# Graph attention on one core: the last two batches of a scatter, summed chunk by chunk or two chunks in turn on column groups of the PE

## The chip, the cores and the metric

The kernel runs on one core of a Trainium2 chip. The metric is the device time of one launch in microseconds (us). Engines are named as in the profile: PE multiplies matrices (PEld is its weight load), DVE and ACT work on vectors, POOL issues the gathers, SP issues other transfers. PE writes only to PSUM, DVE and ACT read it. The PE's clock is throttled, and the profile lists the share of it that was granted.

## The reference

One layer of graph attention on 12500 nodes and 412500 edges, sorted by their target node `dst`, self loops included. With H = 4 heads of 32 values:

```
h   = relu(layernorm(x)) @ W_node.T            per node, 4 x 32
e   = edge_attr @ W_edge.T                     per edge, 4 x 32
att = leaky(sum(concat(h[src], h[dst], e) * a))
m   = max(segment_max(att, dst), 0)
ex  = exp(att - m[dst])
den = segment_sum(ex, dst) + (E - degree) * exp(-m)
out = x + segment_sum(ex / den[dst] * h[src], dst)
```

All is float32. The change concerns the last sum, of weighted rows `ex * h[src]` into the rows of their targets.

## The kernel before

**Chunks and batches.** The sorted edges are cut in 461 chunks of 896 edges (7 tiles of 128; the last chunk has 3 tiles). Eight chunks make a batch; there are 58 batches (`NBT`), numbered 0 to 57, and the last one has 5 chunks. A table in memory holds for each node its projected row, 140 values (4 heads x 35) and 4 more. `gather` (L495) fetches the rows of a batch's source nodes with one indirect transfer per tile into `hs`, from POOL, a batch ahead of the arithmetic.

**What is done with a batch.** `begin` (L509) makes the scores `z` on PE (L518, L521) and the matrices `hot` on DVE (L533): for each tile, 128 edges x 32, a one where an edge's target is the row of that number in the chunk's window of 32 nodes. `weigh` (L537) makes the exponentials `ex_ps` on DVE and ACT (L549 to L564), with a running maximum. `scatter` (L567) multiplies the gathered rows by them on DVE (L578, one instruction of 128x924 values per chunk) and sums them on PE (L586): `hot` of a tile is the stationary operand, the weighted rows are the moving one, and the tiles of a chunk accumulate in PSUM. In batches 0 to 55 three chunks share a matmul (96 x 420), of which only the diagonal blocks are used. In the last two batches, 56 and 57 (`step` 1), each chunk has its own matmuls, 32 x 140, 7 of them, in a PSUM tile `pa` of its own. The name `pa` has two buffers, which are taken in turn; a third tile has to wait until the first was read. A float32 matmul stands in the trace as two records, with two weight loads.

**Collecting and merging.** `collect` (L592) copies each chunk's 32 x 140 block as four blocks of 32 x 35, a head each, from PSUM into `r`: on ACT (L609), and for the last chunk of the last batch on DVE and ACT in turn (L607, L609). `merge` (L611) then scales and scans the chunks of one batch (of two batches, further ahead) on DVE and ACT and adds the result to `acc`. Where nodes are complete, `finish` (L696) divides, brings the four heads together with 16 small matmuls (L721) and stores rows. Those matmuls go to four column groups in turn: each has `tile_position=(0, s * W)`, and writes the PSUM rows `s * W` to `s * W + 31` for s = 0 to 3.

**What sets the order.** The order of instructions on each engine is that of the program (`manual_schedule`). In the main loop, round b issues `load` and `gather` of batch b + 1, `weigh` and `scatter` of b, `begin` of b + 1, `merge`, and `finish` of the nodes that are done. Waits between engines are placed by the framework from the tiles that the instructions read and write. At the end stand `scatter` of 56, `begin` of 57, `merge` and `finish`, then `weigh`, `scatter`, `merge` and `finish` of 57. Constants: `W` = 32 rows a window, `H` = 4, `AW` = 35, `HB` = 33, `G` = 3, `T` = 7.

Of the kernel before, what the change touches and what calls it, by code (L numbers as in the profile page):

```python
# [9 lines left out]
F32 = mybir.dt.float32  # L10
# [7 lines left out]
P = 128  # L18
# [4 lines left out]
H = 4  # L23
HD = D // H
T = 7
# [6 lines left out]
NBT = -(-NCH // CB)  # L32
# [6 lines left out]
W = 32  # L39
G = 3  # L40
# [7 lines left out]
AW = HD + 3  # L48
# [9 lines left out]
def tiles_of(sc):  # L58

    return [T if c < NCH - 1 else LAST for c in (2 * sc, 2 * sc + 1) if c < NCH]  # L60
# [8 lines left out]
def merge_of(b):  # L69

    return next((i, j) for i, j in merges() if i <= b <= j)


def chunks_of(first, last):

    return min((last + 1) * CB, NCH) - first * CB
# [23 lines left out]
def kernel(  # L100
# [12 lines left out]
    nc = tc.nc  # L113
# [28 lines left out]
    q0 = const.tile([1, NC2], I32, name="q0")  # L142
# [18 lines left out]
    sums = const.tile([W, 1], F32, name="sums")  # L161
# [16 lines left out]
    with (  # L178
# [179 lines left out]
        pa = pps.tile([P, 2 * H], F32, name="pw", bufs=1)  # L358
# [4 lines left out]
        k = -2  # L363
# [41 lines left out]
        for k in range(2):  # L405
            for g in range(NG):
                n = min(P, NC2 - g * P)
# [35 lines left out]
        for a in range(4):  # L443
            r = slice(a * W, (a + 1) * W)
# [7 lines left out]
    ps = stack.enter_context(tc.tile_pool(name="ps", bufs=1, space=bass.MemoryType.PSUM))  # L452
# [10 lines left out]
    hot = work.tile([P, T, CB, W], F32, name="hot")  # L463
# [103 lines left out]
    def scatter(s):  # L567


        by_chunk = s.hs[:, :, :EROW].rearrange("p (q t) k -> p q t k", t=T)  # L570
        held = [n for j in range(SB) for n in tiles_of(s.b * SB + j)]
        step = G if s.b + 2 < NBT else 1
        for q0 in range(0, s.chunks, step):
            w = min(step, s.chunks - q0)
            for q in range(q0, q0 + w):
                n = held[q]
                rows = by_chunk[:, q, :n, :].rearrange("p t (h k) -> p t h k", h=H)[:, :, :, :HB]
                nc.vector.tensor_tensor(  # L578
                    rows, rows, ex_ps[:, :n, q * H:(q + 1) * H, None].to_broadcast([P, n, H, HB]), op=OP.mult)
            pa = ps.tile([P, G * H * AW], F32, name="pa", bufs=2)  # L580

            n = held[q0 + w - 1]
            order = [0, *range(n, T if w > 1 else n), *range(1, n)]
            for i in order:
                v = w if i < n else w - 1
                nc.tensor.matmul(pa[:v * W, :v * H * AW], hot[:, i, q0:q0 + v, :].rearrange("p q r -> p (q r)"), by_chunk[:, q0:q0 + v, i, :],  # L586
                                 start=(i == order[0]), stop=(i == order[-1]))
            collect(s, q0, w, pa)

    merged = {}  # L590

    def collect(s, q0, w, pa):  # L592

        first, last = merge_of(s.b)
        if s.b + 2 < NBT and q0 + w == s.chunks:
            nc.scalar.copy(sums, pa[:W, 0:1])  # L596
        if s.b == first and q0 == 0:
            n = chunks_of(first, last)
            r = work.tile([P, AW * (MC + 1)], F32, name="r")
            merged["r"] = r[:, :AW * (n + 1)].rearrange("p (d c) -> p d c", d=AW)  # L600
        for q in range(w):
            at = 1 + (s.b - first) * CB + q0 + q
            for h in range(H):
                to = merged["r"][h * W:(h + 1) * W, :, at]
                k = (q * H + h) * AW
                if s.b == NBT - 1 and q0 + w == s.chunks and h % 2:
                    nc.vector.tensor_copy(to, pa[q * W:(q + 1) * W, k:k + AW])  # L607
                else:
                    nc.scalar.copy(to, pa[q * W:(q + 1) * W, k:k + AW])  # L609

    def merge(c0, n):  # L611

# [124 lines left out]
    def batch(b):  # L737
        if b not in batches:
            s = batches[b] = Batch()
            s.b = b  # L740
            s.chunks = min(CB, NCH - b * CB)
        return batches[b]

    stores = []
    with tc.manual_schedule():
        for b in range(-1, NBT):
# [9 lines left out]
            if b >= 0:  # L756
                s = batch(b)
                weigh(s)
                if b + 1 < NBT:
                    load_pen(batch(b + 1))  # L760
                for store in stores:
                    store()
                stores.clear()
                scatter(s)
# [19 lines left out]
    ps = stack.enter_context(tc.tile_pool(name="rest_ps", bufs=1, space=bass.MemoryType.PSUM))  # L784
# [245 lines left out]
```

## Time and profile before

| what | us |
|---|---|
| five runs, median (lowest to highest) | 5148.1 (5136.21 to 5148.47) |
| the profiled execution | 5140.35 |
| its span | 5138.6 |
| PE busy in the span | 1940.1 (38%) |
| DVE busy | 1807.8 (35%) |
| ACT busy | 645.7 (13%) |
| POOL busy | 3081.7 (60%) |
| first product of batch 56 (L578) starts | 5069.06 |
| first product of batch 57 (L578) starts | 5110.13 |
| last store issued (L731) | 5130.52 |

The span is the time from the first to the last recorded instruction or transfer of one profiled execution; the rest of that execution's time lies around it. Busy shares are averages over stages with different limits. "Idle before, releaser" in a row tells how long the engine had rested and what ended most of that rest; "issue" is time in which the profile shows nothing that it waited for.

### The profile page before, as it was taken

The numbers are of one execution on the slowest core, as the hardware profiler recorded it, in microseconds if no ns is written. First come the engines' busy times: TensorE is split into PE (matmuls) and PEld (weight loads), VectorE is DVE, ScalarE is ACT, GpSimd is POOL, SyncE is SP. The second block draws the span as 40 slices with busy tenths as digits, with TensorE's granted clock in tenths as the row PEclk, the third lists the DMA queues.
The fourth block names the chain that finished last, engine by engine and source line by source line (L and its number), as shares of the span: only waits on it lengthen the run. The fifth ranks groups of instructions, "written<-read, shape, count | busy, mean of one in ns | idle before, by whom it ended". The sixth has DMA issues, their size and how long they took to land.

```text
span 5138.6 us, 24120 instructions
## 1 busy us (share of the span) xinstructions
PE 1940.1 (38%) x4721; PEld 693.8 (14%) x4721; DVE 1807.8 (35%) x3336; ACT 645.7 (13%) x2553; POOL 3081.7 (60%) x3337
## 2 busy tenths in 40 slices
PE   5243424333244144243341442442424414424343
PEld 3011101111011011111110110111101101101112
DVE  6233334233143242322341433423323424233235
ACT  4111111111011011011110111111101101111111
POOL 4676647656656566566566564665665655656662
PEclk8565656566566566665665665666656656656566
DMA  6323323323223233223232222332332323222321
GB/s 177 94 79 90 96 71 92 98 69 90 84 82 89 66 98 93 72 76 100 69 99 72 89 82 63 100 97 69 88 87 68 101 68 95 78 82 84 96 79 48
DMA packets 243628, 440.90 MB, mean 86 GB/s; under 512 B 93946, under 2 KB 144118, under 8 KB 243478
## 3 DMA queue, kind: packets, MB, share of 16 engines
q0 software_dynamic: 103136, 237.83, 17.8%
q1 hardware_dynamic: 127030, 194.11, 11.4%
q10 hardware_dynamic: 13312, 7.36, 0.5%
q8 instruction: 45, 0.74, 0.1%
q14 instruction: 105, 0.86, 0.1%
HBM read 423.75 MB, written 15.29 MB: 85 GB/s over the span
## 4 chain that ended last, share of the span: by engine, by line
another core or an unknown queue 41%; issue 19%; PE 14%; POOL 12%; DVE 9%; ACT 4%; DMA 1%; DVEq 0%; ACTq 0%; POOLq 0%
POOL hs L500 11%; PE pa L586 9%; PE z L518 3%; ACT r L609 2%; DVE hs L578 1%; PE z L521 1%; PE up L721 1%; DMA hs<-table,src 1%; DVE acc L656 1%; DVE z L549 1%; DVE hot L533 1%; DVE up L553 1%; DVE m L555 1%; ACT a L550 0%
## 5 line engine op out<-in xcount | busy, mean ns | idle before, releaser
L500 POOL DMA_INDIRECT hs<-table,src x3223 | 3056.1, 948 | 1009.6 <-issue 976.5
L586 PE MATMUL pa<-hs,hot 128*96 128x420 f32 (+2 forms) x2526 | 1005.2, 567 | 2063.0 <-issue 1946.1
L533 DVE TENSOR_TENSOR hot<-exr,key 128x448 f32<-128x448 f32 x231 | 138.6, 622 | 1987.6 <-remote 1257.2
L586 PEld LDWEIGHTS pa<-hs,hot 128*96 128x96 f32 (+2 forms) x2526 | 460.7, 187 | 2628.1 <-issue 2538.0
L518 PE MATMUL z<-eft,wa 128*32 128x384 f32 (+1 forms) x928 | 526.1, 653 | 676.6 <-issue 655.0
L609 ACT COPY r<-pa 32x35 f32<-32x35 f32 x1842 | 385.2, 209 | 2451.1 <-remote 1255.5
L498 POOL COPY gate<-sums 32x1 f32<-32x1 f32 x56 | 10.0, 178 | 903.1 <-ACT sums L596 903.1
L578 DVE TENSOR_TENSOR hs<-hs,exr 128x924 f32<-128x924 f32 x461 | 476.8, 1102 | 0.0
L521 PE MATMUL z<-mem,twb 128*32 128x512 f32 x464 | 313.9, 799 | 197.9 <-issue 193.0
L726 DVE TENSOR_TENSOR xg<-up,xg 128x448 f32<-128x448 f32 (+2 forms) x30 | 16.4, 588 | 761.0 <-remote 758.2
L518 PEld LDWEIGHTS z<-eft,wa 128*32 128x32 f32 x928 | 102.7, 115 | 1057.5 <-issue 1057.5
L550 ACT ACTIVATE a<-z 32x224 f32<-32x224 f32 x232 | 80.5, 347 | 1308.1 <-DVE z L549 1021.2
L549 DVE TENSOR_TENSOR z<-z,zst 32x224 f32<-32x224 f32 x232 | 89.7, 387 | 240.2 <-PE z L521 144.0
L559 ACT ACTIVATE both<-a 32x224 f32<-32x224 f32 x232 | 89.9, 388 | 370.1 <-DVE a L556 199.0
L513 DVE TENSOR_TENSOR mem<-mem,exr 128x896 f32<-128x896 int32 x116 | 120.3, 1074 | 19.7 <-issue 19.7
L521 PEld LDWEIGHTS z<-mem,twb 128*32 128x32 f32 x464 | 61.2, 134 | 457.6 <-issue 444.4
L656 DVE TENSOR_TENSOR acc<-acc,a 128x70 f32 x461 | 108.9, 236 | 33.1 <-issue 15.6
L553 DVE TENSOR_TENSOR_SCAN up<-pen,z 32x896 f32<-32x896 f32 x58 | 117.0, 2017 | 2.0
L555 DVE TENSOR_TENSOR_SCAN m<-pen,up 32x896 f32<-32x896 f32 x58 | 116.4, 2007 | 2.0
L721 PE MATMUL up<-a,ident 128*32 128x224 f32 (+2 forms) x480 | 44.2, 543 | 190.4 <-issue 98.0
L561 DVE SCALAR_TENSOR_TENSOR both<-pen,m 32x224 f32<-32x224 f32 x232 | 89.9, 388 | 4.7 <-issue 2.3
L551 DVE TENSOR_TENSOR z<-z,a 32x896 f32<-32x896 f32 x58 | 63.0, 1087 | 24.0 <-issue 14.1
(140 smaller groups left out, 792.5 us busy)
## 6 DMA issues: line engine op xcount, KB each, us to landing
eft<-in_ef SPq DMA_DIRECT2D x58, 1792.0 KB
mem<-in_dstc SPq DMA_DIRECT2D x116, 448.0 KB
hs<-table,src POOLq DMA_INDIRECT x3223
twb<-table SPq DMA_DIRECT2D x464, 0.5 KB
pen<-pens SPq DMA_DIRECT2D x58, 112.1 KB
xg<-in_x SPq DMA_DIRECT2D x14, 448.0 KB
table<-rows ACTq DMA_DIRECT2D x9, 648.0 KB
out<-xg SPq DMA_DIRECT2D x13, 448.0 KB
```

The costliest lines, as they stand in the source:

```text
L500: nc.gpsimd.indirect_dma_start(out=s.hs[:, i, :], out_offset=None, in_=table[:, :], in_offset=bass.IndirectOffsetOnAxis(ap=s.src[:, i:i + ...
L513: nc.vector.tensor_tensor(s.mem[:, k, :], s.mem[:, k, :].bitcast(I32), nid_ps[:, pair:pair + 1].to_broadcast([P, CE]), op=OP.is_equal)
L518: nc.tensor.matmul(s.z[:, part], wa3[:, j, :], s.eft[:, j, part], start=(j == 0), stop=False)
L521: nc.tensor.matmul(s.z[:, part], twb[:, s.b % 2, k, :], s.mem[:, k, part], start=False, stop=(k == 1))
L533: nc.vector.tensor_tensor(hot[:, :, q0:q0 + 2, :].rearrange("p t q r -> p q t r"), rows_ps[:, None, None, :].to_broadcast([P, 2, T, W]), k ...
L549: nc.vector.tensor_tensor(grouped(s.z, g), grouped(s.z, g), zst[g * R:(g + 1) * R, :, :], op=OP.add)
L553: nc.vector.tensor_tensor_scan(up, s.pen[:, :CE], s.z, 0.0, op0=OP.add, op1=OP.max)
L555: nc.vector.tensor_tensor_scan(m[:, ::-1], s.pen[:, CE:0:-1], up[:, ::-1], 0.0, op0=OP.add, op1=OP.max)
L578: nc.vector.tensor_tensor(rows, rows, ex_ps[:, :n, q * H:(q + 1) * H, None].to_broadcast([P, n, H, HB]), op=OP.mult)
L586: nc.tensor.matmul(pa[:v * W, :v * H * AW], hot[:, i, q0:q0 + v, :].rearrange("p q r -> p (q r)"), by_chunk[:, q0:q0 + v, i, :], start=(i ...
L609: nc.scalar.copy(to, pa[q * W:(q + 1) * W, k:k + AW])
L656: nc.vector.tensor_tensor(cols, cols, put[:, i0 + i, :, :], op=OP.add)
```

## The change

In the last two batches the chunks are taken two at a time. Both products (L578) come first. Then the tiles of the two chunks are multiplied in turn: tile 0 of the first chunk, tile 0 of the second, tile 1 of the first and so on. Chunk q uses the column group q mod 4, so it writes PSUM rows of its own (32 (q mod 4) onward), and the columns of slot q // 4. One PSUM tile holds a whole batch: it is allocated once instead of once a chunk. After a pair, `collect` copies both blocks, eight copies of 32 x 35. `collect` now takes a list of blocks instead of the tile; for the other batches this names the same values as before, save that the copy that gates the gathers (`sums`, one column) reads the last block instead of the first.

```diff
-        step = G if s.b + 2 < NBT else 1
+        single = s.b + 2 >= NBT
+        step = 2 if single else G
+        if single:
+            one = ps.tile([P, G * H * AW], F32, name="pa", bufs=2)
+            by_slot = one[:, :2 * H * AW].rearrange("p (j k) -> p j k", j=2)
         for q0 in range(0, s.chunks, step):
...
+            if single:
+
+                for i in range(T):
+                    for q in range(q0, q0 + w):
+                        if i < held[q]:
+                            g = q % 4
+                            nc.tensor.matmul(by_slot[g * W:(g + 1) * W, q // 4, :], hot[:, i, q, :], by_chunk[:, q, i, :],
+                                             start=(i == 0), stop=(i == held[q] - 1), tile_position=(0, g * W))
+                collect(s, q0, w, [by_slot[q % 4 * W:(q % 4 + 1) * W, q // 4, :] for q in range(q0, q0 + w)])
+                continue
             pa = ps.tile([P, G * H * AW], F32, name="pa", bufs=2)
...
-            collect(s, q0, w, pa)
+            collect(s, q0, w, [pa[q * W:(q + 1) * W, q * H * AW:(q + 1) * H * AW] for q in range(w)])
...
-    def collect(s, q0, w, pa):
+    def collect(s, q0, w, blocks):
...
-            nc.scalar.copy(sums, pa[:W, 0:1])
+            nc.scalar.copy(sums, blocks[-1][:, 0:1])
...
-                k = (q * H + h) * AW
+                what = blocks[q][:, h * AW:(h + 1) * AW]
                 if s.b == NBT - 1 and q0 + w == s.chunks and h % 2:
-                    nc.vector.tensor_copy(to, pa[q * W:(q + 1) * W, k:k + AW])
+                    nc.vector.tensor_copy(to, what)
                 else:
-                    nc.scalar.copy(to, pa[q * W:(q + 1) * W, k:k + AW])
+                    nc.scalar.copy(to, what)
```

`held[q]` is the number of tiles of chunk q, 7 or, for the last chunk, 3.

## The prediction on record

> **What bounds the kernel now.** I began with the page. Over the whole span the chain that ended last is gathers on POOL and their transfers, which the change doesn't touch; it touches `scatter` and `collect` in the last two batches of 58 only. Page, the span and the two costliest groups concerned:
>
> ```profile
> span 5138.6 us, 24120 instructions
> L586 PE MATMUL pa<-hs,hot 128*96 128x420 f32 (+2 forms) x2526 | 1005.2, 567 | 2063.0 <-issue 1946.1
> L609 ACT COPY r<-pa 32x35 f32<-32x35 f32 x1842 | 385.2, 209 | 2451.1 <-remote 1255.5
> ```
>
> The group mixes three forms, so what the change is worth must be read from its stage. The chain of waits, cut to 5069-5093 us (start, length, what), has batch 56 in it:
>
> ```profile
> 5069.20 0.96 DVE hs L578
> ...
> 5070.41 15.15 PE pa L586 x112
> ...
> 5085.58 0.21 ACT r L609
> ```
>
> So in batch 56 PE's matmuls bound the stage: 8 chunks x 7 tiles, two records each (x112). The last four copies and the merge on DVE follow. In batch 57 the same chain holds `PE pa L586` from 5111.33 us. The last gather is issued by 5056 us, so a microsecond won or lost here is one of the kernel. The timeline of the stage (start, length, instruction, count) gives the unit prices:
>
> ```profile
> 5069.06 8.28 DVE L578 TENSOR_TENSOR hs<-hs,exr 128x924 f32<-128x924 f32 x8
> 5070.41 15.14 PE L586 MATMUL pa<-hs,hot 128*32 128x140 f32 x112 [51.01 <-DVE hs L578]
> 5073.89 0.88 ACT L609 COPY r<-pa 32x35 f32<-32x35 f32 x4 [5.75 <-PE pa L586]
> 5075.57 0.88 ACT L609 COPY r<-pa 32x35 f32<-32x35 f32 x4 [0.81 <-PE pa L586]
> ```
>
> DVE weighs a chunk each 1.03 us, PE sums one each 1.67 us (the pitch of the copies), ACT moves one out in 0.88 us and then idles 0.8 us. The copies of one chunk lie beside the matmuls of the next, since each chunk has a `pa` buffer of its own. The first chunk takes 3.48 us because the granted clock is low. Stretches of 3.41 us (length, PE busy and records, clock, DMA share, GB/s) show how it moves:
>
> ```profile
> 4445.71:4449.12 3.41, 1.44 (x5) 1.00 0.23 52
> 4449.13:4452.53 3.40, 2.16 (x9) 1.00 0.25 65
> 431.63:435.04 3.41, 1.39 (x4) 1.00 0.24 65
> 435.05:438.45 3.40, 1.04 (x3) 0.50 0.21 56
> 5070.35:5073.75 3.40, 3.34 (x15) 0.50 0.28 83
> 5073.76:5077.17 3.41, 3.41 (x31) 1.00 0.02 5
> ```
>
> After 1.44 us busy of 3.41 the clock stayed at 1.00, after 1.39 us it fell to 0.50, and a full stretch raised it.
>
> **The change, part by part.** 56 + 31 matmuls, 32 + 20 copies and 8 + 5 products keep their number and form. What moves is the order, the rows written and the buffer.
>
> (1) *Two chunks in turn on two column groups.* No L586 row of before has two groups at work. The nearest rows are those of `finish` (L721), whose 16 matmuls go to four groups in turn:
>
> ```profile
> 5095.13 1.00 PEld L721 LDWEIGHTS up<-a,ident 128*32 128x32 f32 x32 [1.26 <-issue]
> 5095.16 1.29 PE L721 MATMUL up<-a,ident 128*32 128x160 f32 x32 [0.59 <-DVE a L714]
> ```
>
> At the pitch of L586 (1.67/14 = 0.119 us a record of 140 columns) 32 records of 160 columns in a row would take 32 x 0.119 x 160/140 = 4.4 us; they took 1.29. Four streams thus run side by side. I take two streams of L586 as running fully side by side: a warm pair takes what a chunk took. Bounds: no overlap at all, 28 records in a row (rival B), and none cheaper than one stream, as each group still has its 14 records. The trace of L721 is the nearest, same weight width and data type.
>
> The Trainium skill speaks against this: "TensorE: Matmul & The Clock Gate", Part 3 (packing small matmuls), says that a weight load overlaps matmuls in flight only if its row group differs, and here all groups share the rows. The 32 weight loads above lie within 1.00 us beside running matmuls, so the row decides. By the rule the sum would be rival B's.
>
> (2) *A buffer per batch.* `one` is allocated once, so no matmul waits for a fresh buffer; but the built program of the changed kernel has a new wait: the first matmul of each later pair waits for ACT's semaphore at the value that the **eighth copy of the pair before** sets, although other rows or columns are written. So copies no longer lie beside matmuls: PE, then ACT, then PE. Such a handover exists in before, where a third group waits for the first group's copies (chain of waits, 4918-4936 us):
>
> ```profile
> 4932.22 0.22 ACT r L609
> 4932.44 0.04 issue
> 4932.48 3.52 PE pa L586 x14
> ```
>
> It costs 0.05 us. Behind the waiting matmul on PE stand the rest of the batch, then batch 57's `z` (L518, L521) or the last `finish` (L721).
>
> The same skill's "TensorEngine Tiling (Array Packing)", section "PSUM Bottleneck", warns that tiling speeds up TensorE but not the emptying of PSUM. The rows agree: 8 copies of 0.22 us are 1.76 us a pair against 1.67 us of matmuls. By that rule alone, with both side by side, the sum would be rival D's.
>
> (3) *Both products ahead of the pair.* The second chunk's first matmul stands behind the second product, and everything after it in PE's order too. The second product ends at about 5071.18; with the 0.24 us that PE took after the first one, PE goes on at 5071.42 instead of at once. DVE's order and its own end are as before.
>
> *Batch 56, step by step.* A warm burst of 14 records is 13 x 0.119 + 0.28 (one record's length) + 0.03 to the copy = 1.86, with the second stream's start 1.87 us. Pair 1: from 5071.42, 10 records at the low clock's 0.233 us ((3.48-0.44-0.03)/13) up to the rise at 5073.76, the rest at 0.119: copies start at 5074.43, end at 5076.19. Then three times 0.05 + 1.87 + 1.76 = 3.68: 5079.87, 5083.55, **5087.23**. Before, the last copy ended at 5085.58 + 0.88 = 5086.46. So **+0.8 us**. PE ends at 5085.4, before at 5085.5, so `z` of batch 57 is no later; its reader on DVE is. Cover lost: none.
>
> *Batch 57.* Before, from PE's first matmul at 5111.33 to the last copy's end at 5121.68: 10.35 us. After, counted from the start: copies of pair 1 from 4.02 to 5.78, pair 2 7.70 and 9.46, the odd chunk (3 tiles, 6 records: 5 x 0.119 + 0.31 = 0.91 after 0.05) 10.42, its four copies by ACT and DVE in turn 0.93 (5120.75 to 5121.68): 11.35. **+1.0 us.**
>
> *Clock.* Between bursts PE now rests 1.85 us of every 3.68. A stretch of 3.41 us then holds at least 1.56 us of work, above the 1.44 that kept the clock up, so it holds once it is up. But whether pair 1 raises it depends on where the stretches lie: there is 0.4 us less work in the first one. Started 0.8 us later, batch 57's pair 1 fills only some 2.2 of its first 3.41 us, and pair 2 may run low too: 3.48 instead of 1.87 for it and 0.44 for pair 1, together +2.0 us. Sum: **+1.8 us** with the clock as now, **+3.8** with a late rise in batch 57. I take **+3**, since other executions place the stretches otherwise. On the profiled execution's own 5140.35 us (span 5138.6 and 1.75 around it) that is 5143; the runs shown lie from 5136.2 to 5148.5 with a median of 5148.1, and nothing ahead of 5070 us changes, so on the median it is **5151 us**.
>
> **Rivals.**
> (B) *The streams don't overlap: slower.* A pair is then 28 records in a row, 3.52 us warm: +1.65 for each of four warm pairs and 1.4 for each pair 1, so +9.4, with the +1.8 **+11.2 us, 5159**. For it: each matmul has a semaphore step of its own, those of L721 only the last. Against: L721's 1.29 us. It takes the kernel over 0.2% once a pair costs 1.5 us more, 3.4 in all. Chance 0.07.
> (C) *The clock stays low or falls back* in the pauses, place: pairs 2 to 4 and batch 57. Four pairs x 1.6 + 2 x 0.44 + 0.7 for the odd chunk = +8.0, with 1.8 **+9.8, 5158**; up to 1 more where `z` starts low. It decides where a stretch holds less than about 1.4 us of work. Against: the 1.56. Chance 0.16.
> (D) *The new wait is harmless, copies lie beside the next pair: faster.* Then ACT bounds batch 56: 5074.43 + 4 x 1.76 = 5081.5, 5.0 less than before; batch 57 4.02 + 3.52 + 0.93 = 8.5, 1.9 less: **-6.9, 5141**. Against: the wait is in the program. Chance 0.07.
>
> **Numbers.** Forecast 0.70, B 0.07, C 0.16, D 0.07. A measurement of this kernel tells about 0.2%, 10.3 us, from no change. The forecast and D lie within it, B is over it, C is on the edge. The shown runs alone differ by 12 us, so I leave some chance to either side: faster 0.05, same 0.82, slower 0.13. Range: from the lowest run shown, 5136, to the slowest rival on the highest run, 5161.
>
> **What would show it.** In the profile after: ACT rows of x8 copies about 3.7 us apart, each PE burst starting 0.05 us after a copy and waiting "<-ACT"; bursts of 28 records of 1.8 us (right) or 3.5 us at clock 1.00 (B); clock 0.50 in 5078-5085 (C); bursts starting before the copies end (D). The prediction is wrong if anything ahead of 5070 us moves.

## The result, and the profile after

The changed kernel takes **5165.2 us** in the median (5143.4 to 5177.1) where the kernel before, run beside it, takes 5148.1 (5134.8 to 5157.4): a ratio of 1.0033, 95% interval 1.0027 to 1.0039. That is 17 us more; forecast were 3 us more, 5151, with a range up to 5161. The profiled execution took 5174.61 us.

The sets of runs below were each made on one chip, with runs of the kernel before beside them, and are compared only within a set: before took 5099, 5098 and 5105 us in three of them, but 4164 and 4165 in two, for a reason that experiment 5 shows in part. Times are medians; a ratio with its interval is an estimate of its own from the same runs and can lie 0.15% beside the ratio of the medians.

The page after, its span and two groups (out<-in, count, busy us, mean ns, idle before and its releaser; the kernel's lines have moved, L609 is now L623 and L726 of `finish` is L740):

```profile
span 5172.8 us, 24113 instructions
...
L623 ACT COPY r<-pa 32x35 f32<-32x35 f32 x1842 | 385.5, 209 | 2459.5 <-remote 1474.7
...
L740 DVE TENSOR_TENSOR xg<-up,xg 128x448 f32<-128x448 f32 (+2 forms) x30 | 16.4, 588 | 784.1 <-remote 781.3
```

The span is 34.2 us longer than before's 5138.6. The first product of batch 56, which starts at 5069.06 in before, starts here at 5099.69: **30.6 us are lost ahead of the changed code**, and 3.6 in it. First the 3.6. The timeline of batch 56 (start, length, instruction, count, idle before and its releaser):

```profile
5106.75 1.93 PE L590 MATMUL pa<-hs,hot 128*32 128x140 f32 x28 [1.85 <-ACT r L623]
5108.72 1.79 ACT L623 COPY r<-pa 32x35 f32<-32x35 f32 x8 [2.02 <-PE pa L590]
5110.56 1.93 PE L590 MATMUL pa<-hs,hot 128*32 128x140 f32 x28 [1.88 <-ACT r L623]
5112.53 1.76 ACT L623 COPY r<-pa 32x35 f32<-32x35 f32 x8 [2.02 <-PE pa L590]
```

This is what was forecast: 28 records in 1.93 us, so two streams run side by side, and then PE rests while ACT copies, by the releaser `<-ACT`. In batch 57 the second pair is slow, as feared. The stretches of its two pairs (length, PE, PEld, DVE, ACT, POOL busy with counts, clock, DMA share, GB/s):

```profile
5143.95:5147.46 3.51, 3.48 (x26) 2.38 (x26) 2.48 (x3) 0.00 (x0) 0.00 (x0) 0.50 0.02 5
5149.27:5152.57 3.30, 3.22 (x28) 2.33 (x28) 0.00 (x0) 0.00 (x1) 0.00 (x0) 0.57 0.00 0
```

28 records took 3.22 us; by the trace's clock records the clock rose from 0.50 to 1.00 only 2.8 us after the first of them had started. From a batch's first product to its last copy's end, batch 56 takes 18.41 us (before 17.40), batch 57 14.50 (11.55); from the first product of 56 to the end it is 73.15 (69.52).

Now the 30.6. The starts of POOL's copy `gate<-sums` (L498), one a batch, tell where they are. Nearly all batches without a `finish` are 80 to 81 us long in both kernels. The 13 batches with a `finish` sum to 1390.6 us in before and to 1418.3 in after, 27.7 of the 30.6. In them DVE waits long ahead of `finish`'s sum. The page of before shows it in a row, and shows in the chain's shares how much of the time went to such waits; the prediction passed over both:

```profile
another core or an unknown queue 41%; issue 19%; PE 14%; POOL 12%; DVE 9%; ACT 4%; DMA 1%; DVEq 0%; ACTq 0%; POOLq 0%
...
L726 DVE TENSOR_TENSOR xg<-up,xg 128x448 f32<-128x448 f32 (+2 forms) x30 | 16.4, 588 | 761.0 <-remote 758.2
```

758.2 us of waiting in 13 batches, 58 each, for something that the profile can't name ("remote"); in after 781.3. These 13 waits are a third of the chain's 41%, 714 of 2084 us. The rest lies mostly ahead of ACT's copies (L609, 718 us) and of DVE's `hot` (L533, 535 us). The timeline of one batch that differs much, before and then after:

```profile
1366.38 3.21 PE L721 MATMUL up<-a,ident 128*32 128x224 f32 x32 [14.42 <-DVE a L714]
1420.48 1.16 DVE L726 TENSOR_TENSOR xg<-up,xg 128x448 f32<-128x448 f32 x2 [54.25 <-remote]
```

```profile
1368.63 3.22 PE L735 MATMUL up<-a,ident 128*32 128x224 f32 x32 [14.11 <-DVE a L728]
1430.10 1.16 DVE L740 TENSOR_TENSOR xg<-up,xg 128x448 f32<-128x448 f32 x2 [61.62 <-remote]
```

The sum waits for its own load, which has landed long before, and for PE's semaphore from the last of the 16 matmuls. The semaphore events of the trace show the latter late: the matmuls of 1366.38 end, by their rows, at 1369.59, but the increment comes at 1420.46, and DVE starts 0.02 us after it. In 12 of the 13 batches it comes 51 to 59 us after the last matmul starts, in the 13th 35. In 11 of 13 it comes 5.4 to 7.0 us after the start of POOL's last gather instruction of the batch (in the other two 0.9 and 18.6 us ahead of it); in after 6.2 to 7.3 us after it in 12 of 13.

The Trainium skill bears on this row: "Perfetto Trace Analysis", section "Tensor Engine Instruction (MATMUL, LD_WEIGHTS)", says that a matmul's end in the profile is computed, and that its semaphore goes out only when PSUM has acknowledged the write. The rows agree that the end shown is no release; no run here shows whether the acknowledgement is what was late.

### The profile page after: what moved, and what is told of

It reads as the page before. It is cut to its first block, busy times and chain, and to the rows that moved or that the text cites. A ratio compares the mean times of both kernels' runs of the same rounds, so it can differ in the third digit from the quotient of the medians.

```text
span 5172.8 us, 24113 instructions
## 1 busy us (share of the span) xinstructions
PE 1929.6 (37%) x4721; PEld 686.0 (13%) x4721; DVE 1807.1 (35%) x3336; ACT 651.1 (13%) x2553; POOL 3071.8 (59%) x3337
## 4 chain that ended last, share of the span: by engine, by line
another core or an unknown queue 41%; issue 20%; PE 15%; DVE 10%; POOL 8%; ACT 4%; DMA 1%; DVEq 0%; ACTq 0%; POOLq 0%
PE pa L600 9%; POOL hs L500 8%; PE z L518 3%; ACT r L623 3%; DVE hs L582 2%; PE z L521 1%; DMA hs<-table,src 1%; PE up L735 1%; DVE acc L670 1%; DVE up L553 1%; DVE m L555 1%; DVE z L549 1%; DVE hot L533 1%; ACT a L550 1%
## 5 line engine op out<-in xcount | busy, mean ns | idle before, releaser
L600 PE MATMUL pa<-hs,hot 128*96 128x420 f32 (+1 forms) x2352 | 986.0, 589 | 2031.4 <-issue 1925.4
L533 DVE TENSOR_TENSOR hot<-exr,key 128x448 f32<-128x448 f32 x231 | 138.4, 622 | 1969.4 <-remote 1499.3
L600 PEld LDWEIGHTS pa<-hs,hot 128*96 128x96 f32 (+1 forms) x2352 | 441.2, 193 | 2591.7 <-issue 2477.9
L623 ACT COPY r<-pa 32x35 f32<-32x35 f32 x1842 | 385.5, 209 | 2459.5 <-remote 1474.7
L498 POOL COPY gate<-sums 32x1 f32<-32x1 f32 x56 | 9.9, 177 | 943.3 <-ACT sums L610 943.3
L521 PE MATMUL z<-mem,twb 128*32 128x512 f32 x464 | 308.4, 782 | 194.2 <-issue 194.0
L740 DVE TENSOR_TENSOR xg<-up,xg 128x448 f32<-128x448 f32 (+2 forms) x30 | 16.4, 588 | 784.1 <-remote 781.3
L549 DVE TENSOR_TENSOR z<-z,zst 32x224 f32<-32x224 f32 x232 | 89.8, 387 | 244.6 <-PE z L521 148.4
L521 PEld LDWEIGHTS z<-mem,twb 128*32 128x32 f32 x464 | 60.8, 133 | 453.6 <-issue 441.6
```

The source lines that it names most:

```text
L521: nc.tensor.matmul(s.z[:, part], twb[:, s.b % 2, k, :], s.mem[:, k, part], start=False, stop=(k == 1))
L533: nc.vector.tensor_tensor(hot[:, :, q0:q0 + 2, :].rearrange("p t q r -> p q t r"), rows_ps[:, None, None, :].to_broadcast([P, 2, T, W]), k ...
L549: nc.vector.tensor_tensor(grouped(s.z, g), grouped(s.z, g), zst[g * R:(g + 1) * R, :, :], op=OP.add)
L623: nc.scalar.copy(to, what)
```

## The experiments

**Theory.** One edit outside the last two batches was left uncosted: the copy `sums`, which opens the gate of the gathers, reads the last block of its tile. Theory 1: this makes the loss ahead of batch 56. Rival, theory 2: the read is as cheap as its row (0.150 us against 0.148) and the loss has another cause.

### 1. The read alone, and the change without it

```diff
 before_late_sums (on before)
-            nc.scalar.copy(sums, pa[:W, 0:1])
+            nc.scalar.copy(sums, pa[(w - 1) * W:w * W, (w - 1) * H * AW:(w - 1) * H * AW + 1])
 after_first_sums (on after)
-            nc.scalar.copy(sums, blocks[-1][:, 0:1])
+            nc.scalar.copy(sums, blocks[0][:, 0:1])
```

> The kernel before with one edit: the one-column copy `sums`, which opens the gate of the gathers in batches 1 to 55, reads the last block of its tile (rows 32 to 63) as the changed kernel does, and not the first. Theory 1, the moved read of `sums` is what costs time ahead of the last two batches: changed minus before is +17 in the medians and the tail accounts for +3.6, so this kernel is +13.5 us, 5161.5, and the 13 batches with a finish are about 1 us longer each. Theory 2, the read costs only what its record shows (0.150 us against 0.148) and the loss is not from this edit: 55 x 0.002 = 0.1 us, 5148, no change.

> The changed kernel with that one read put back to the first block (rows 0 to 31), so that only the last two batches differ from before. Theory 1 (the read costs what is lost ahead of the tail): +3.6 us on before, 5152, and 13.5 less than the changed kernel. Theory 2 (the loss ahead does not come from the read): still +17, 5165. In both the tail, from the first product of batch 56 to the end of the span, is 73.1 us as in the changed kernel, with the clock up to 2 us either way.

Measured: before_late_sums 5119.9 us against 5098.7, **1.0049** (1.0034 to 1.0065); after_first_sums 5094.0, 0.9984 (0.9964 to 1.0004). The edit of one column's read costs 21 us by itself, and without it the change costs nothing that shows; its 3.6 us in the tail lie just outside the interval, which is 20 us wide, and its own tail was 71.82 us, 2.3 more than before's. Theory 1 holds, theory 2 falls. The 21 us are more than the 13.5 expected, which came from the first set.

Why would it? In an ordinary batch the two kernels differ in one place, the copy behind `sums`. ACT's timeline in before and in before_late_sums, at the same batch:

```profile
2043.41 0.15 ACT L596 COPY sums<-pa 32x1 f32<-32x1 f32 x1 [7.40 <-remote]
2043.47 1.75 ACT L609 COPY r<-pa 32x35 f32<-32x35 f32 x8
```

```profile
2042.11 0.15 ACT L596 COPY sums<-pa 32x1 f32<-32x1 f32 x1 [6.71 <-remote]
2042.28 1.75 ACT L609 COPY r<-pa 32x35 f32<-32x35 f32 x8
```

The first copy starts 0.06 us after `sums` where both read the first block, 0.17 us where `sums` has read the last (in after 0.18). So the eight copies and `merge` stand 0.12 us later in their batch, while the gate opens as before: `merge`'s first reading of `r` (L621) starts 1.62 us after `gate<-sums` in before and 1.75 in before_late_sums, in the mean of the 13 batches. Of that less reaches `finish`: its matmuls start 15.50 to 15.57 us after `gate<-sums` in three profiles where the copy follows at 0.06 us, 15.61 to 15.62 in five where it follows at 0.17.

### 2. The order of blocks or the read itself

Theory P: it is this order. Rival R: reading rows 32 to 63 into the gate costs in itself. Both kernels let the last group's copies begin with the last block:

```diff
-        for q in range(w):
+        gated = s.b + 2 < NBT and q0 + w == s.chunks
+        for q in reversed(range(w)) if gated else range(w):
```

late_sums_last_first is before_late_sums with this, first_sums_last_first is before with this.

> before_late_sums (the gate's read of the last block, measured 21 us slower than before) with one more edit: of the copies that follow `sums` in the last group of a batch, those of the last block come first, so that the copy behind `sums` reads the rows that `sums` has just read. Theory P, the order of blocks on ACT: in before the first copy starts 0.06 us after `sums`, in before_late_sums, where it turns back to the first block, 0.18 us after; the eight copies, merge and finish's matmul are 0.12 us later and the wait of finish for its matmul ends later. By it the copy follows at 0.06 us again and the kernel is like before, within 6 us. Theory R, reading rows 32 to 63 into the gate costs by itself: again 15 to 25 us slower than before.

> The kernel before, `sums` reading the first block as there, but the copies of the last group with the last block first. Theory P (see late_sums_last_first): `sums` and the copy behind it now read different blocks, the copy starts 0.18 us after `sums` and not 0.06, and the kernel is 15 to 25 us slower than before, like before_late_sums. Theory R: the read is as in before, so no change, within 6 us.

Measured, against 5097.5: late_sums_last_first 5096.5, **1.0006** (0.9987 to 1.0025); first_sums_last_first 5119.3, **1.0057** (1.0037 to 1.0078). ACT's timelines, in this order:

```profile
2003.44 0.15 ACT L596 COPY sums<-pa 32x1 f32<-32x1 f32 x1 [6.71 <-remote]
2003.50 1.76 ACT L610 COPY r<-pa 32x35 f32<-32x35 f32 x8
```

```profile
2037.85 0.15 ACT L596 COPY sums<-pa 32x1 f32<-32x1 f32 x1 [8.10 <-remote]
2038.02 1.76 ACT L610 COPY r<-pa 32x35 f32<-32x35 f32 x8
```

Time follows the order, not the block: 0.06 us and no loss, 0.17 us and 22 us lost. P holds, R falls.

### 3. The wait of finish

If the loss arises in that wait, a kernel without the wait has neither the wait nor the loss. `finish_later` calls `finish` a batch later, between `scatter` and `begin`; `finish_split` puts its part up to the matmuls ahead of `scatter` and its two sums behind `scatter`'s products; `finish_split_late_sums` adds the read of the last block.

```diff
 finish_later
                 scatter(s)
+            for b0, n, behind in parts():
+                if behind == b - 1 and b < NBT - 1:
+                    stores.append(finish(work, ps, "up", em_ps, b0, n))
             if b + 1 < NBT:
                 begin(batch(b + 1))
...
-                if behind == b:
+                if behind == b and b >= NBT - 2:
 finish_split
...
+                late = [finish(work, ps, "up", em_ps, b0, n) for b0, n, behind in parts() if behind == b - 1 and b < NBT - 1]
                 scatter(s)
+                for add, store in late:
+                    add()
+                    stores.append(store)
...
```

> The kernel before with `finish` called one batch later, between scatter and begin, for all parts but the last two: its matmuls then come right after a gather and not in the midst of one. In before its sum on DVE waits 58 us in 12 of 13 such batches for the semaphore of its last matmul, which arrives about 6 us after the last gather instruction of the batch, and these batches take 108 us where the others take 80 to 81. Theory A, the matmul's end is held up only while gathers run on POOL: the batches with a finish fall to 82 to 86 us, 13 x 22 to 26 = 290 to 340 us less, 4810 to 4860. Theory B, the wait is for something of finish itself (its load, its own matmuls): the wait moves along, 58 us between two gathers, and the kernel is the same or up to 13 x 30 = 390 us slower.

> The kernel before with finish one batch later and in two halves, for all parts but the last two: its steps up to the 16 matmuls stand ahead of scatter, its two sums on DVE behind scatter's products, so that scatter's matmuls follow on PE and DVE has work before it needs the result. In finish_later the wait of finish fell from 58 to 5 us, but z, then the last matmul ahead of a pause of PE, came 46 us late, and the batch behind was 86 to 99 us. Theory C, during the gathers the semaphore of the last matmul ahead of a pause is held up, not that of one that others follow: no wait of tens of us is left but those hidden by the gathers, all batches are 80 to 84 us, 13 x 25 to 28 = 325 to 365 us less than before, 0.930 to 0.937 of it. Theory D, every matmul's semaphore is held up during gathers: the sums on DVE wait till the gather ends, hidden or not, and the gain is that of finish_later, 0.97, or less.

> finish_split with the gate's read of the last block. If what the moved read costs in before_late_sums (21 us) arises in finish's wait for its matmul, and finish_split has no such wait left, the moved read is free here: the same as finish_split within 5 us, save 55 x 0.002. If it costs in every batch, 15 to 25 us slower than finish_split.

Measured: finish_later 4952.8 against 5098.7, 0.9714 (0.9687 to 0.9742), half of what theory A expected. Its timeline, after a gate that opens at 2056.60, shows why:

```profile
2060.29 3.02 PE L721 MATMUL up<-a,ident 128*32 128x224 f32 x32 [31.00 <-DVE a L714]
...
2067.94 1.16 DVE L726 TENSOR_TENSOR xg<-up,xg 128x448 f32<-128x448 f32 x2 [7.70 <-remote]
...
2119.82 0.39 DVE L549 TENSOR_TENSOR z<-z,zst 32x224 f32<-32x224 f32 x1 [45.30 <-issue]
```

`finish`'s matmuls, 4 us after the gate, are released 5 us late. The matmuls of `z` (L521) end at 2073.47, 17 us after it, and DVE's L549, which waits for PE's semaphore from them, starts 46 us later. So it is no property of `finish`. finish_split took **4884.9 against 5097.5, 0.9595** (0.9569 to 0.9620), 213 us less:

```profile
1993.23 3.22 PE L721 MATMUL up<-a,ident 128*32 128x224 f32 x32 [27.44 <-DVE a L714]
2043.54 1.16 DVE L727 TENSOR_TENSOR xg<-up,xg 128x448 f32<-128x448 f32 x2 [42.52 <-PE pa L586]
```

The semaphore is late here too, by 47 to 50 us, although `scatter`'s matmuls follow on PE: theory C falls. The trace's semaphore events show that the increments of other matmuls are held up with it, as theory D has it. The last matmul of 1993.23 and 14 of `scatter` raise the same semaphore and end, by their rows, from 1996.44 to 2042.96, but no increment comes between 1965.80 and 2043.51; then 15 come 0.04 us apart. The trace of before has 44 such bursts of 4 to 8, nearly all in batches without a `finish`; that of late_sums_again (experiment 5) has none. So it is not `finish` alone that waits. Yet most of its wait now lies beside the gathers, the batch takes 88 us and not 108, and the gain is larger than theory D expected. finish_split_late_sums took 4890.4, 0.9604 (0.9578 to 0.9629): of the 21 us that the read costs in before, 5.5 are left, where the five runs of either kernel spread over 9 to 10 us. So most of the cost arises where `finish`'s wait is exposed.

### 4. The tail: the shared tile, and the turns

`tile_per_pair` allocates `one` for each pair, from the two buffers in turn, and not once a batch. `tile_per_pair_first_sums` adds the read of the first block. `chunk_by_chunk` exchanges the two loops of after:

```diff
 chunk_by_chunk
-                for i in range(T):
-                    for q in range(q0, q0 + w):
+                for q in range(q0, q0 + w):
+                    for i in range(T):
```

> The changed kernel with a tile of `pa` for each pair of chunks, two in turn, so that the copies of one pair may lie beside the matmuls of the next. If the one shared tile is what makes PE wait for the eighth copy, the waits of 1.85 us ahead of each later pair go: pair 2 of batch 56 starts at once, ACT with 1.76 us a pair becomes the bound, and batch 56 is 5 us and batch 57 1.9 us shorter than before, as rival D had it: the tail is 62.6 to 65 us where the changed kernel has 73.1 and before 69.5; the total is 8 to 10.5 us less than the changed kernel, 5155 to 5157. If PE waits for the copies all the same, 5165.

> tile_per_pair with the gate's read put back to the first block, so that nothing ahead of batch 56 differs from before and the copies of one pair lie beside the matmuls of the next. tile_per_pair has shown a tail of 64.1 us where before has 69.5 and the changed kernel 73.2, and about 15 + 5 us lost ahead of it. If that loss is the read's, this kernel is 5.4 us faster than before (0.999 of it, at the edge of what can be told); if the loss comes with the column groups in some other way, 15 us slower.

> The changed kernel with the matmuls of a pair in order of chunks and not in turn; column groups, tile and copies as there. It asks whether the two streams overlap because neighbouring matmuls have different groups. If so, a warm pair takes 28 x 0.119 = 3.3 to 3.5 us from its first matmul to its copies where the changed kernel takes 1.93, and the tail is 3 x 1.5 + 1.5 to 3 us longer: 79 to 81 us. If the groups do not matter or the second stream runs beside the first all the same, 1.9 us a pair and a tail of 73.

tile_per_pair has a tail of **64.10 us**, where before has 69.52 and after 73.15. PE no longer waits for copies, and ACT copies without a rest (104 records in one burst, 16 copies in a row, and 0.19 us later the other 16):

```profile
5045.40 8.74 PE L588 MATMUL pa<-hs,hot 128*32 128x140 f32 x104 [0.18 <-DVE hs L579]
5048.91 3.60 ACT L621 COPY r<-pa 32x35 f32<-32x35 f32 x16 [6.61 <-PE pa L588]
```

In all it took 5113.5, 1.0037 (1.0021 to 1.0052): the read's cost hides the gain. With the read put back, tile_per_pair_first_sums took 4160.5 against 4164.2, 0.9990 (0.9981 to 0.9999). This version is 4 us ahead of before where the semaphore is not held up; it had no run where it is, and none beside the changed kernel. Where it is held up, finish_split is the fastest kernel with right sums that was run. chunk_by_chunk has bursts of 3.08 us, a tail of 78.71 (expected 79 to 81) and 4171 us in one run beside 4164:

```profile
4098.88 3.08 PE L590 MATMUL pa<-hs,hot 128*32 128x140 f32 x28 [1.85 <-ACT r L623]
4102.00 1.79 ACT L623 COPY r<-pa 32x35 f32<-32x35 f32 x8 [3.17 <-PE pa L590]
```

So the streams overlap because neighbours have different column groups, and with them PSUM rows of their own: 28 records take 1.93 us in turn, 3.08 in order. The Trainium skill, "TensorE: Matmul & The Clock Gate", Part 3, lets a weight load overlap matmuls in flight only where the row group differs; these rows do not keep to that, and the measurement decides. The same part lists column packing too, three column tiles with a speedup of 2.38 (here two, 3.08 to 1.93 us), so it does not speak for rival B as the prediction has it.

### 5. What holds the semaphore up

In the set of runs with tile_per_pair_first_sums the kernel before took 4164 us. In the profile of tile_per_pair_first_sums all batches are 70.0 to 70.6 us apart, as 56 gathers of 1.25 us make them, and `finish`'s semaphore comes 0.4 to 0.6 us after its last matmul starts. What held it up elsewhere was absent. It stayed open whether the read costs there, and whether POOL's gathers are the cause where it is held up. `rows_in_order` leaves the gathers out: SP loads rows of the table in order into the same tiles, so its sums are not those of the graph:

```diff
-            nc.gpsimd.indirect_dma_start(
-                out=s.hs[:, i, :], out_offset=None, in_=table[:, :],
-                in_offset=bass.IndirectOffsetOnAxis(ap=s.src[:, i:i + 1], axis=0))
+            nc.sync.dma_start(s.hs[:, i, :], table[i * P:(i + 1) * P, :])
```

`finish_three` (on tile_per_pair_first_sums) has `finish`'s steps up to the weights ahead of `scatter` and its matmuls and sums behind `begin`.

> The kernel before with the gathers left out: the same tiles are loaded by SP with 128 rows of the table in order, so the sums are not those of the graph; the bytes into the tiles are the same. It asks what holds up the semaphore of finish's last matmul. If it is the gathers that POOL issues, the wait of 58 us ahead of finish's sum on DVE goes: its first sum follows the last matmul within 1 us, and z and scatter's matmuls run without gaps. If it is the traffic into the tiles, or something of finish's own matmuls, a wait of tens of us stays. The total is of no interest.

> tile_per_pair_first_sums with finish in three parts, one batch later: its steps on ACT and DVE up to the weights stand ahead of scatter, its 16 matmuls and the two sums behind begin, that is behind the matmuls of z, some 5 us after the gate has opened. In finish_split the matmuls stood 25 us into the gathers, their semaphore came 46 to 49 us late and the batch took 88 us; in finish_later, 4 us into the gathers, it came 5 us late, but z behind it 46 us. If early in the gathers a semaphore is not held up, finish costs DVE some 10 us that the gathers hide, all batches are 80 to 83 us: 13 x 26 us = 340 us less than before, and 5 for the tail, 0.932 of it. If it is held up from there on as well, weigh waits 50 us and the kernel is like before or like finish_later, 0.97 to 1.0.

> before_late_sums once more. Where the kernel before takes about 5100 us (semaphores held up during the gathers): 15 to 25 us slower than before, as measured. Where it takes about 4164 us (batches of 70 us, set by the 56 gathers of 1.25 us): the copies are 0.12 us later, but the gate is then opened 35 us ahead of the end of the gathers before, so no change, within 2 us. If the read costs in both, it is not the wait of finish that makes it.

> rows_in_order once more: the gathers are left out, SP loads rows of the table in order into the same tiles, and the sums are not those of the graph. Where the kernel before takes about 5100 us: if POOL's gathers are what holds up finish's semaphore, the sum on DVE follows the last matmul within 1 us and the kernel takes the 2857 us that it took where before took 4164; if not, a wait of tens of us stays in each of 13 batches and it is over 3100 us. Where before takes 4164 us: 2857 us, which tells nothing.

> finish_three once more (finish in three parts, a tile of `pa` for each pair, the gate's read in the first block). Where semaphores are held up during the gathers: 13 x 26 = 340 us and 5 for the tail less than before, 0.932 of it, if early in the gathers they are not; 0.97 to 1.0 if they are. Where they are not held up: 0.999, as measured.

> tile_per_pair_first_sums once more (only the last two batches differ from before, two tiles of `pa` in turn). 5.4 us less than before by the tails of 64.1 and 69.5 us, wherever it runs: 0.9990 of 5100 or 0.9987 of 4164.

> The changed kernel as it is. Where the kernel before takes about 4164 us, late_sums_again has shown the moved read of `sums` to cost nothing, so only the tail is left: the forecast of this study, +1.8 to +3.8 us, 1.0004 to 1.0009 of before, 4166 to 4168. Where before takes about 5100 us: +3.6 for the tail and 15 to 25 for the read, 1.0033 to 1.0055. Were the change to cost 17 us in itself, 4181.

> rows_in_order once more: gathers left out, rows in order loaded by SP. Where before takes about 5100 us: 2857 to 2865 us if POOL's gathers are what holds up the semaphores, and the sum of finish follows its last matmul within 1 us; over 3100 us if not. Where before takes 4164 us, it tells nothing.

Where before took 4164 to 4165 us: late_sums_again 4164.3, **1.0000** (0.9991 to 1.0009); first_sums_pair_again 4160.4 and finish_three_again 4160.4, 0.9992 (0.9983 to 1.0001) both; finish_three 4159.8, 0.9990. The read is free there, the better tail is worth 4 us, and the place of `finish` nothing. rows_in_order and rows_in_order_again took 2857 and 2865 us. What DVE waited for ahead of `finish`'s sum (L726) in late_sums_again (releaser, us, times):

```profile
  PE up L721: 46.6, 15
```

46.6 us in 15 waits, 3.1 each, which is what the matmuls themselves take; the profile can now name the releaser. In before it was 758.2 in 13.

The last set fell where before took 5104.8. changed_again took 5131.5, **1.0054** (1.0030 to 1.0077), at the upper end of what was expected. rows_in_order_third took 2865 us, as where nothing is held up, and its sum follows at once:

```profile
998.80 3.21 PE L719 MATMUL up<-a,ident 128*32 128x224 f32 x32 [6.60 <-DVE a L712]
1002.07 1.16 DVE L724 TENSOR_TENSOR xg<-up,xg 128x448 f32<-128x448 f32 x2 [3.42 <-PE up L719]
```

The load on the transfers was no lighter around it than in before's wait, as two windows show (rows_in_order_third, then before):

```profile
1000.00:1010.00 10.00, 2.02 (x24) 0.79 (x16) 6.12 (x9) 1.39 (x4) 0.00 (x0) 0.67 0.68 243
```

```profile
2062.50:2119.00 56.50, 0.00 (x0) 0.00 (x0) 0.00 (x0) 0.00 (x0) 39.19 (x42) 0.53 0.21 56
```

243 GB/s and no wait, against 56 GB/s and 57 us of it. So what holds PE's semaphore up goes with the gathers that POOL issues, and not with the amount of traffic into the tiles. The edit takes away three things together: POOL as the issuer, the indirect addresses and the scattered rows. Which of them does it was not tested.

## Why the prediction was wrong, point by point

- *Two streams side by side*: right. A warm pair takes 1.97 us to its first copy, forecast 1.87.
- *PE waits for the eighth copy*: right. The handover takes 0.05 us, forecast 0.05; pairs are 3.79 us apart, forecast 3.68.
- *Batch 56, +0.8*: +1.0. *Batch 57, +1.0, and up to +2.0 for the clock*: +2.95, with the late rise. *Tail, +3 of +1.8 to +3.8*: +3.6 in the profiled execution. In another of the changed kernel (changed_again) the tail was 75.47 us, 2.3 more, with pair 2 slow in both batches (3.22 and 3.46 us), and in after_first_sums 71.82. So the range was a little narrow, and a forecast of +3 that fits one profile is in part luck: the tail depends on where the clock's stretches fall.
- *Rival B* fell to the 1.93 us; chunk_by_chunk shows its price, 78.71. *Rival C* came true only in part: the clock kept up in batch 56 and rose late in 57. What spoke against it was too sure: the 1.44 us that "kept the clock up" are one row, and in before itself the clock fell after stretches with 1.52 to 1.54 us of PE (1936.91 to 1940.32 and 4305.76 to 4309.17 us), so 1.56 left no margin. *Rival D*, -6.9, is what tile_per_pair does: -5.4.
- **"Nothing ahead of 5070 us changes"** is the step that failed. The read of `sums` moves in 56 batches, has no term in the sum, and was by its row worth 0.1 us. It moved the copies behind it by 0.12 us, and this cost some 17 - 3.6 = 13 us in the first runs and 21 in the second, most of it in the 13 batches where nothing covers `finish`'s wait. The prediction read the chain of waits as gathers and transfers; its largest share, 41%, was waits of unknown cause, and a third of them were the waits of `finish` that come behind this edit.
- *The range, 5136 to 5161*: its upper end by its own terms, rival B's +11.2 on the highest run of 5148.5, is 5160. The 5165.2 lie above either.

What stays open: why a start 0.12 us later makes the wait 1 to 2 us longer in a batch. The semaphore's time varies anyway (from 26 us ahead of the start of the batch's last gather to 7 after it, in the profiles of kernels that call `finish` where before does), and a mean over the 13 batches from one profile moves by as much as the effect: 103.4, 105.4 and 107.0 us where the copy follows at 0.06 us, 105.8 to 109.1 in five profiles where it follows at 0.17. So that the later start lengthens the wait is argued from where the cost arises, not seen in single batches. Open too: why gathers hold the semaphore up on some chips and not on others, whether recording the executions has a part in it, and finish_three where they do, which had no run there.

## What to carry to other kernels

Cost every line of a diff, the ones in passing too: list what runs in the stages that the change isn't meant to touch, and what order of blocks or rows it moves there. A large "unknown" share in the chain of waits is the first thing to name: look up in the semaphore events which release came late, because work just ahead of such a wait costs far more, or less, than its row. When buffers are merged to save one, ask which wait the extra buffer had hidden: with one tile the tail was 3.6 us longer than before, with two in turn 5.4 shorter.

## What the runs showed of the hardware

- A semaphore of PE can come 35 to 59 us after its matmul while POOL issues gathers (before and after), and 0.6 us after it when SP loads the same tiles (rows_in_order_third); held-up increments then come together, 0.04 us apart (15 in finish_split). In two sets of runs the profiles show none late, and the same program took 4164 us and not 5148.
- On ACT a copy starts 0.06 us after the start of a copy of 0.15 us that read the same block of PSUM, and 0.17 us after the start of one that read another block.
- Matmuls of 32 columns of weights on two column groups in turn: 28 records of 140 columns in 1.93 us, in order 3.08.
